# Expert work on pairs of chunks with 256-column operands, in a graph layer with a mixture of experts

## The chip, the cores and the metric

The kernel runs on one core of a Trainium2 chip. The core has a matrix engine (TensorE, in the profile PE for its matmuls and PEld for its weight loads), VectorE (DVE), ScalarE (ACT), GpSimd (POOL), a queue engine (SyncE, SP), a software-addressed on-chip memory (SBUF) and a small accumulator memory for matmul results (PSUM). The metric is the device time of one execution in microseconds (us). Smaller is better.

## The reference

The input is `x` of 6250 nodes by 256 features and 100,000 directed edges (`src`, `dst`), sorted by `dst`. Two layers are added to `x`, one after the other:

```python
# layer 1: graph neighbours
h       = layernorm(x)
msg_sum = segment_sum(h[src], dst, num_segments=n)
deg     = segment_sum(ones, dst, num_segments=n)
agg     = msg_sum / max(deg, 1)
x       = x + concat([h, agg]) @ W.T + b
# layer 2: mixture of 8 experts, each token goes to its best 2
xn      = layernorm(x) * gamma + beta
top     = top_k(xn @ Wr + br, 2);  w = softmax(top)
for e in range(8):
    hid = gelu(xn @ W1[e] + b1[e])        # 256 -> 512
    y  += (hid @ W2[e] + b2[e]) * w_full[..., e]   # 512 -> 256
x       = x + y
```

All is in float32.

## The kernel before

**Edges.** The kernel first computes `z = layernorm(x) @ W_agg` and a few more columns for all nodes and stores it to `z_d` in device memory. The edges come as 784 tiles of 128 edges. For each tile, POOL fetches the 128 rows of `z_d` that the sources name, with one indirect DMA (`gather`, L601), into one of a ring of `XG` = 28 buffers `xg`. VectorE makes a 0/1 matrix `hot` which says to which node of the window each edge goes (L612, seven tiles at once), and TensorE multiplies both into the accumulator `pS` (`add_edges`, L618). Fourteen tiles (`C`) make a window, and there are 56 windows (`W`). At a window's end ACT copies `pS` out (`keep_sums`, L640). The gather of tile t + `XG` is written straight after tile t's matmul, so the ring is filled as far ahead as it is long, and POOL waits when TensorE has not yet read the slot.

**Chunks.** Four windows (`CW`) form a chunk; there are 14 chunks, in batches of 8, 5 and 1 (`BATCHES`). After a chunk's last window a chain of steps, `window_done`, is spread over the next 56 tiles by due times (`Steps`, `LateSteps` for chunks 10 to 12, `LastSteps` for chunk 13): the second layer norm, the routing, counts and ranks, a sort by matmuls with 0/1 matrices (`sort_tokens`, L705, with the evictions L708), `copy_runs` (L859), and `find_rows` (from L805), which works out where each token's two results will be. `copy_runs` puts the sorted tokens into the chunk's slots in the buffer `xe`: 128 slots per expert, and what does not fit goes to overflow slots of the batch. There are two slot buffers of `HS` columns, for even and odd chunks, and the copies are 448 in all, four per expert and chunk. `xe` is `SC` = 5056 columns wide.

**Experts.** `start_experts` turns a chunk into tasks (`expert_stages`). Two experts share a task group: `hidden` (L884) does W1 times the slots, 2 x 8 matmuls of 128 columns, in two tasks, and the gelu (L889) on 128 columns each; `result` (L897) does hidden times W2, 2 x 4 matmuls of 256 columns, the bias add (L901) and the store to `y_d` (L903). After a batch's last chunk come the tasks of its overflow tiles (`more_stages`, L927, L936, L945). A chunk has 64 hidden and 32 result matmuls. A float32 matmul shows as two passes in the profile.

**Order.** The kernel's text decides the order on each engine. After each edge tile `after(t)` runs the steps that are due, adds a pace to an account (0.72 nominal us per tile; 0.6 in the last 56 tiles; 1.2 or 2.0 in the turns behind the last tile) and takes tasks from the list while the account is above zero; a hidden task counts 2.0 and a result task 1.75. `sum_rows` handles the output: for each of 49 node tiles a load of the layer-1 result (L973), two gathers from `y_d` on POOL (L976), two weighted adds on VectorE (L983) and a store (L985). It starts in the last `XG` tiles, in slots of the ring that are no longer needed, three per node tile, and only for a batch whose experts are all done; at most `XG // 3 - 1` adds are pending.

Of the kernel before, what the change touches and what calls it, by code (L numbers as in the profile page):

```python
# [8 lines left out]
F32 = mybir.dt.float32  # L9
I32 = mybir.dt.int32  # L10
AF = mybir.ActivationFunctionType
ALU = mybir.AluOpType
# [5 lines left out]
P = 128  # L18
EPS = 1e-5
C = 14  # L20
TB = 4
UB = 2
CW = 4
CAP = 64
BATCHES = (8, 8), (5, 5), (1, 2)
GB = 3
LATE = 40
XG = 28
RAW = 1
LATE_CHUNKS = 4  # L30

# [2 lines left out]
def gnn_ffn_kernel(ctx: ExitStack, tc: tile.TileContext, x, x_cols, src, dst, dst_next, gw, gw_t, gb, gb_cols, gamma, beta,  # L34
# [35 lines left out]
    nc = tc.nc  # L70
    N, D = x.shape
    NX, H = w1.shape[0], w1.shape[2]
    KD, KH = D // P, H // P
# [3 lines left out]
    W = src.shape[1]  # L77
# [4 lines left out]
    SH = P  # L82
    HS = NX * SH + CAP
    XS = P + CAP
    SC = 2 * HS + XS * sum(n for _, n in BATCHES)

    class Group:
        pass
# [2 lines left out]
    batches = []  # L91
    for n, tiles in BATCHES:
        B = Group()
        B.first, B.n, B.tiles = sum(b.n for b in batches), n, tiles
        B.at = HS + XS * sum(b.tiles for b in batches)
        B.row = batches[-1].end_row if batches else 0
        B.more_row = B.row + n * NX * SH
        B.end_row = B.more_row + XS * tiles
        B.left = n * NX * SH // (2 * P) + tiles
        batches.append(B)  # L100
# [3 lines left out]
    ps = ctx.enter_context(tc.tile_pool(name="ps", bufs=2, space=PSUM))  # L104
# [3 lines left out]
    y_d = dram.tile([batches[-1].end_row, D], F32, name="y_d")  # L108
# [734 lines left out]

    def copy_runs(K, e):
        if e == 0:
            assert K.index < 2 or Ks[K.index - 2].left == 0
        lowest = min(K.at, K.batch.at)
        _, v = nc.values_load_multi_w_load_instructions(
            K.runs[0:1, e].rearrange("o j t -> o (j t)"), engines=(ET.Activation,),
            min_val=0, max_val=SC, skip_runtime_bounds_check_because="clamped to it")  # L850
        for j in range(CW):
            to_at = nc.s_assert_within(v[2 * j], lowest, K.last,
                                       skip_runtime_bounds_check_because="behind the base, and clamped")
            src_at = nc.s_assert_within(v[2 * j + 1], 0, 2 * P,
                                        skip_runtime_bounds_check_because="a window has so many at most")
            whole = xs[:, j * KD * 2 * P:(j + 1) * KD * 2 * P + CAP]
            src = bass.AP(tensor=whole.tensor, offset=whole.offset,
                          ap=[whole.ap[0], [2 * P, KD], [1, 2 * P + CAP]])
            nc.scalar.activation(xe[:, :, bass.ds(to_at, CAP)], src[:, :, bass.ds(src_at, CAP)], AF.Copy)  # L859
# [5 lines left out]
    def in_turn(items, of):  # L865

        return [(us, f, of) for t in range(len(items) + 2) for d in range(3)
                if 0 <= t - d < len(items) and d < len(items[t - d]) for us, f in items[t - d][d]]

    def expert_stages(K):  # L870

        B = K.batch

        def hidden(U, h):

            if h == 0:
                U.hid = slots.tile([P, KH, 2 * P], F32, name="hid")
            ph = ps.tile([P, KH // 2, 2 * P], F32, name="ph")
            for i in range(KH // 2):
                c = h * KH // 2 + i  # L880
                for a in range(2):
                    at = K.at + (U.e + a) * SH
                    for k in range(KD):
                        nc.tensor.matmul(ph[:, i, a * SH:(a + 1) * SH], w1_sb[:, U.e + a, k, c * P:(c + 1) * P],  # L884
                                         xe[:, k, at:at + SH], start=(k == 0), stop=(k == KD - 1))
            for i in range(KH // 2):
                c = h * KH // 2 + i
                for a in range(2):
                    nc.scalar.activation(U.hid[:, c, a * SH:(a + 1) * SH], ph[:, i, a * SH:(a + 1) * SH],  # L889
                                         AF.Gelu, bias=b1_sb[:, U.e + a, c:c + 1])  # L890

        def result(U, h):

            if h == 0:
                U.py = ps.tile([P, 2, D], F32, name="py", bufs=1)
            for c in range(KH):
                nc.tensor.matmul(U.py[:, h, :], U.hid[:, c, h * P:(h + 1) * P], w2_sb[:, U.e + h, c, :],  # L897
                                 start=(c == 0), stop=(c == KH - 1))
            if h == 1:
                ys = slots.tile([P, 2, D], F32, name="rows", bufs=3)  # L900
                nc.vector.tensor_tensor(ys, U.py, b2_sb[:, U.e:U.e + 2, :], op=ALU.add)  # L901
                at = K.row + U.e * SH
                nc.sync.dma_start(y_d[at:at + 2 * P, :].rearrange("(t p) d -> p t d", p=P), ys)  # L903
                K.left -= 1
                B.left -= 1

        items = []
        for e in range(0, NX, 2):
            U = Group()
            U.e = e  # L910
            items.append([[(2.0, lambda U=U, h=h: hidden(U, h)) for h in range(2)],
                          [(1.75, lambda U=U, h=h: result(U, h)) for h in range(2)]])
        K.left = len(items)
        return in_turn(items, K)

    def more_stages(B):
# [70 lines left out]

    tasks, later, Ks, sums, adds = [], {}, [], [], []  # L990
    slots, w1_sb, w2_sb, xe = None, None, None, None
    now, spent, clock, due, added, spares = None, 0.0, 0.0, 0.0, 0.0, 0
    class Steps:
# [61 lines left out]

    def start_experts(K):
        B = K.batch
        tasks.extend(expert_stages(K))
        if K.index == B.first + B.n - 1:
            tasks.extend(more_stages(B))  # L1060
        Ks.append(K)
        sums.extend((K, n) for n in K.nodes)
# [22 lines left out]
    def after(t):  # L1085
        nonlocal now, spent, clock
        now = t
        while later.get(t):
            later[t].pop(0)()
        later.pop(t, None)  # L1090
        clock += 0.6 if t < W * C else 0.3 if tasks else 1.2

        pace = 0.6 if W * C - 56 <= t < W * C else 0.72 if t < W * C else 1.2 if len(Ks) < W // CW else 2.0
        spent = min(spent + pace, pace) if tasks else 0.0
        while tasks and spent > 0:
            us, f, _ = tasks.pop(0)
            spent -= us
            clock += us
            f()
        sum_rows()  # L1100
# [15 lines left out]
    for index in range(W // CW):  # L1116
        K = Group()
        K.index, K.first = index, index * CW
        K.batch = next(B for B in batches if index < B.first + B.n)
        K.row = K.batch.row + (index - K.batch.first) * NX * SH  # L1120
        K.at = 0 if index % 2 == 0 else SC - HS
        K.last = max(K.at + HS, K.batch.at + XS * K.batch.tiles) - CAP
        K.count = work.tile([1, 2, CW, NX], F32, name="count")
        G = K.group = Group()
        G.n, G.first, G.x1 = CW, K.first, []
        G.mv = small.tile([P, CW, 2], F32, name="mv4", bufs=2)
        for g in range(K.first, K.first + CW):
            if g > 0:
                V = V_next
            for c in range(C):  # L1130
                t = g * C + c
                add_edges(V, c)
                if c == 0:
                    hot_tiles(V, HC)
                if c == HC and g + 1 < W:
                    V_next = new_window(g + 1, V)
                if t + XG < len(edge_tiles):
                    gather(*edge_tiles[t + XG])
                for to, what in loads[:1]:
                    loads.pop(0)  # L1140
                    nc.sync.dma_start(to, what)
                if u_tasks and t % 2 == 0:
                    u_tasks.pop(0)()
                    if not u_tasks:
                        u_pools.close()
                        slots = fast_pools.enter_context(tc.tile_pool(name="slots", bufs=2))
                        at(t + 60, load_last)
                        xe = slots.tile([P, KD, SC], F32, name="xe", bufs=1)
                        for n in range(4):
                            at(t + 3 + 5 * n, clear_slots, n)  # L1150
                        w1_sb, w2_sb, parts = weights(slots)
                        for n, (to, what) in enumerate(parts):
                            at(t + 2 + 2 * n, nc.scalar.dma_start, to, what)
                if c == HC + 5:
                    load_u(V)
                if c == C - 1:
                    window_done(V, G, K, t)
                after(t)
    t = W * C
# [152 lines left out]
```

## Time and profile before

| what | value |
|---|---|
| time, median of 3 runs | 1426.46 us (1421.05 to 1427.55) |
| profiled execution, its own time | 1418.08 us |
| span of the profiled execution | 1416.3 us |
| mean granted TensorE clock | 0.892 |
| TensorE busy (matmuls) | 1123.6 us, 79% |
| TensorE busy (weight loads) | 903.0 us, 64% |
| VectorE busy | 690.8 us, 49% |
| ACT busy | 460.5 us, 33% |
| POOL busy | 843.9 us, 60% |
| 784 edge tiles end at about | 1256 us |

The span runs from the first to the last instruction; the time of the profiled execution is 1.8 us longer. A line of a group gives the line of code, engine and operation, what is written and read, how often, then busy time, mean duration of one in ns, and the engine's idle time before these instructions with what ended most of it. `issue` means that the engine waited for nothing that the profile shows. The starts of expert work are visible in the timeline; ACT's eviction at L640 marks the end of each window but the last. Busy time of TensorE is modelled for pipelined matmuls, so a busy TensorE is not one at its peak.

### The profile page before, as it was taken

How to read it: one execution, taken by the hardware profiler on the slowest of the kernel's cores; microseconds unless marked ns; L12 is line 12 of the kernel's file. 1: busy time of each engine (PE TensorE's matmuls, PEld its weight loads, DVE VectorE, ACT ScalarE, POOL GpSimd, SP SyncE). 2: the span in 40 equal slices, each digit the busy share in tenths (PEclk: the TensorE clock that was granted, in tenths of full speed). 3: DMA queues.
4: the chain of work that ended last, by engine and by line, in shares of the span. 5: the costliest groups of instructions: out<-in, count | busy, mean ns of one | idle time of the engine just before them, and what ended most of it. 6: DMA issues, size and time to landing. Idle time of an engine off the chain costs nothing. (4 is left out here: it accounts for less than half of the span.)

```text
span 1416.3 us, 18881 instructions
## 1 busy us (share of the span) xinstructions
PE 1123.6 (79%) x5352; PEld 903.0 (64%) x5352; DVE 690.8 (49%) x2433; ACT 460.5 (33%) x1281; POOL 843.9 (60%) x892
## 2 busy tenths in 40 slices
PE   7819957696987879698796969899889897986760
PEld 6718734575766758586675857567767786774650
DVE  6637776163444435354443534555462643656423
ACT  3310003333342333344243323433542343532310
POOL 0256666666666666666666666566656666564543
PEclk9859977898998989899897988999999998997876
DMA  9858895445454454544445454454545453564754
GB/s 331 285 181 269 270 324 157 104 123 122 114 128 113 114 120 117 123 122 120 118 115 112 123 119 115 118 124 115 120 111 133 116 134 103 115 197 139 197 148 126
DMA packets 143578, 210.08 MB, mean 148 GB/s; under 512 B 36652, under 2 KB 111128, under 8 KB 143340
## 3 DMA queue, kind: packets, MB, share of 16 engines
q0 software_dynamic: 42768, 118.91, 34.3%
q1 hardware_dynamic: 92364, 80.45, 18.0%
q10 hardware_dynamic: 8336, 9.45, 2.0%
q8 instruction: 45, 0.74, 0.2%
q14 instruction: 65, 0.53, 0.1%
HBM read 163.86 MB, written 44.86 MB: 147 GB/s over the span
## 5 line engine op out<-in xcount | busy, mean ns | idle before, releaser
L601 POOL DMA_INDIRECT xg<-z_d,src_i x770 | 732.5, 951 | 415.2 <-issue 175.7
L618 PE MATMUL pS<-xg,hot 128*128 128x265 f32 x1568 | 452.4, 418 | 68.8 <-DVE hot L612 33.4
L618 PEld LDWEIGHTS pS<-xg,hot 128*128 128x128 f32 x1568 | 304.8, 204 | 151.7 <-issue 97.5
L884 PE MATMUL ph<-xe,w_sb 128*128 128x128 f32 x1792 | 255.4, 293 | 75.5 <-issue 66.3
L884 PEld LDWEIGHTS ph<-xe,w_sb 128*128 128x128 f32 x1792 | 243.1, 207 | 94.8 <-issue 77.4
L612 DVE TENSOR_TENSOR hot<-cols,rel 128x896 f32<-128x896 f32 x112 | 121.9, 1089 | 275.5 <-PE pS L618 154.3
L897 PE MATMUL py<-w_sb,hid 128*128 128x256 f32 x896 | 223.2, 391 | 28.0 <-issue 16.8
L889 ACT ACTIVATE hid<-ph,b_sb 128x128 f32<-128x128 f32 x448 | 126.4, 374 | 270.4 <-remote 125.5
L897 PEld LDWEIGHTS py<-w_sb,hid 128*128 128x128 f32 x896 | 172.2, 195 | 64.5 <-issue 36.4
L859 ACT ACTIVATE xe<-xs x448 | 139.3, 311 | 86.3 <-issue 36.4
L976 POOL DMA_INDIRECT xg<-y_d,plans x98 | 95.7, 977 | 83.1 <-issue 21.4
L901 DVE TENSOR_TENSOR rows<-py,b_sb 128x512 f32<-128x512 f32 x56 | 38.5, 688 | 168.9 <-PE py L897 62.7
L708 ACT ACTIVATE xs<-pm,beta_sb,gamma_sb 128x256 f32<-128x256 f32 x112 | 57.2, 566 | 169.2 <-PE pm L705 73.7
L705 PE MATMUL pm<-to,xn 128*128 128x256 f32 x224 | 62.5, 403 | 24.6 <-DVE to L698 18.7
L640 ACT ACTIVATE sums<-pS 128x265 f32<-128x265 f32 x55 | 21.4, 389 | 172.1 <-PE pS L618 100.2
L705 PEld LDWEIGHTS pm<-to,xn 128*128 128x128 f32 x224 | 44.1, 201 | 35.6 <-issue 11.6
L271 PE MATMUL ph<-gc,x_t 128*128 128x264 f32 (+1 forms) x200 | 58.8, 420 | 8.2 <-ACT root L180 4.2
L889 ACT ACT_TABLE_LOAD x25 | 32.1, 1283 | 77.8 <-PE pS L618 43.5
L271 PE MATMUL pm<-gc,x_t 128*128 128x264 f32 (+1 forms) x192 | 54.9, 411 | 0.0
L271 PEld LDWEIGHTS ph<-gc,x_t 128*128 128x128 f32 x200 | 40.2, 205 | 18.6 <-ACT root L180 4.6
L983 DVE SCALAR_TENSOR_TENSOR xg<-xg,plans,xg 128x256 f32<-128x256 f32 (+1 forms) x98 | 45.4, 482 | 12.5 <-DMA xg<-y_d,plans 10.9
L660 DVE SCALAR_TENSOR_TENSOR x<-pS,rdeg,x 128x264 f32<-128x264 f32 x55 | 27.1, 493 | 48.1 <-DMA x<-u_d 35.4
(214 smaller groups left out, 873.4 us busy)
## 6 DMA issues: line engine op xcount, KB each, us to landing
y_d<-rows SPq DMA_DIRECT2D x56, 256.0 KB
xg<-z_d,src_i POOLq DMA_INDIRECT x770
w_sb<-w_dram ACTq DMA_DIRECT2D x16, 512.0 KB
x<-u_d SPq DMA_DIRECT2D x55, 132.0 KB
x_d<-x SPq DMA_DIRECT2D x55, 128.0 KB
u_d<-u_t SPq DMA_DIRECT2D x24, 264.0 KB
x_t<-x_cols_dram SPq DMA_DIRECT2D x12, 512.0 KB
xu<-x_dram SPq DMA_DIRECT2D x24, 256.0 KB
```

Of the source, the lines that this page charges most:

```text
L271: nc.tensor.matmul(pz, x_t[:, t, k, :], gc[:, h * KD + k, :n], start=(k == 0), stop=(k == KD - 1))
L601: nc.gpsimd.indirect_dma_start(out=xg[(g * C + c) % XG][:, :DZ], out_offset=None, in_=z_d[:, :], in_offset=bass.IndirectOffsetOnAxis(ap=sr ...
L612: nc.vector.tensor_tensor(hot, col[:, None, :].to_broadcast([P, HC, P]), V.rel[:, c:c + HC, None].to_broadcast([P, HC, P]), op=ALU.is_equal)
L618: nc.tensor.matmul(V.pS, V.hot[c // HC][:, c % HC, :], xg[(V.g * C + c) % XG], start=(c == 0), stop=(c == C - 1))
L705: nc.tensor.matmul(px[:, k, :], G.xn[i][:, k * P:(k + 1) * P], G.one_hot[i], start=True, stop=True)
L708: nc.scalar.activation(xs[:, at:at + 2 * P], px[:, k, :], AF.Identity, bias=beta_sb[:, k:k + 1], scale=gamma_sb[:, k:k + 1])
L859: nc.scalar.activation(xe[:, :, bass.ds(to_at, CAP)], src[:, :, bass.ds(src_at, CAP)], AF.Copy)
L884: nc.tensor.matmul(ph[:, i, a * SH:(a + 1) * SH], w1_sb[:, U.e + a, k, c * P:(c + 1) * P], xe[:, k, at:at + SH], start=(k == 0), stop=(k = ...
L889: nc.scalar.activation(U.hid[:, c, a * SH:(a + 1) * SH], ph[:, i, a * SH:(a + 1) * SH], AF.Gelu, bias=b1_sb[:, U.e + a, c:c + 1])
L897: nc.tensor.matmul(U.py[:, h, :], U.hid[:, c, h * P:(h + 1) * P], w2_sb[:, U.e + h, c, :], start=(c == 0), stop=(c == KH - 1))
L976: nc.gpsimd.indirect_dma_start(out=V.y2[r], out_offset=None, in_=y_d[:K.batch.end_row, :], in_offset=bass.IndirectOffsetOnAxis(ap=plans[:c ...
L983: nc.vector.scalar_tensor_tensor(V.o, V.y2[r], plans.bitcast(F32)[:count, n, 2 + r:3 + r], V.o, op0=ALU.mult, op1=ALU.add)
```

## The change

Chunks 0 to 11 are worked on in six pairs (`PAIRS`), by a new `pair_stages`; chunks 12 and 13 stay alone.

- A pair becomes tasks when its odd chunk's experts start. The even chunk's tasks wait until then, 56 tiles longer than before.
- `hidden` does one expert of both chunks: the 128 slots of the one and the 128 of the other are a single operand of 256 columns in two segments. Per expert that is 8 matmuls of 256 columns, in place of 16 of 128, and 4 gelus of 256 columns in place of 8 of 128. `result` keeps its count and size; its two halves are now the same expert of two chunks, so that the bias is one row for both, and the store is one DMA to two blocks of rows.
- `xe` holds three slot buffers: one for odd chunks, two which even chunks take in turn (chunks 12 and 13 go on in that turn). The overflow slots of the last batch share the place of the first's. `SC` becomes 5760. The ring `XG` goes from 28 to 24 buffers.
- A task counts 1.75, and the pace is 0.8 while more than 16 tasks are waiting, otherwise 0.72, in the tiles before the last 56.

```diff
--- before.py
+++ after.py
@@ -25,7 +25,8 @@
 BATCHES = (8, 8), (5, 5), (1, 2)
 GB = 3
 LATE = 40
-XG = 28
+XG = 24
+PAIRS = 6
 RAW = 1
 LATE_CHUNKS = 4
 
@@ -82,7 +83,10 @@
     SH = P
     HS = NX * SH + CAP
     XS = P + CAP
-    SC = 2 * HS + XS * sum(n for _, n in BATCHES)
+    OVER = 2 * HS
+    RIGHT = OVER + XS * (BATCHES[0][1] + BATCHES[1][1])
+    SC = RIGHT + HS
+    assert len(BATCHES) == 3 and BATCHES[2][1] <= BATCHES[0][1]
 
     class Group:
         pass
@@ -92,7 +96,7 @@
     for n, tiles in BATCHES:
         B = Group()
         B.first, B.n, B.tiles = sum(b.n for b in batches), n, tiles
-        B.at = HS + XS * sum(b.tiles for b in batches)
+        B.at = OVER if len(batches) == 1 else OVER + XS * BATCHES[1][1]
         B.row = batches[-1].end_row if batches else 0
         B.more_row = B.row + n * NX * SH
         B.end_row = B.more_row + XS * tiles
@@ -843,7 +847,8 @@
 
     def copy_runs(K, e):
         if e == 0:
-            assert K.index < 2 or Ks[K.index - 2].left == 0
+            assert K.at not in filled or filled[K.at].left == 0
+            filled[K.at] = K
         lowest = min(K.at, K.batch.at)
         _, v = nc.values_load_multi_w_load_instructions(
             K.runs[0:1, e].rearrange("o j t -> o (j t)"), engines=(ET.Activation,),
@@ -913,6 +918,58 @@
         K.left = len(items)
         return in_turn(items, K)
 
+    def pair_stages(K, L):
+
+        B = K.batch
+        assert L.batch is B and L.at < K.at
+
+        def slots_of_both(k, e):
+
+            own = xe[:, k, L.at + e * SH:L.at + (e + 1) * SH]
+            return bass.AP(tensor=own.tensor, offset=own.offset, ap=[own.ap[0], [K.at - L.at, 2], [1, SH]])
+
+        def hidden(U, h):
+
+            if h == 0:
+                U.hid = slots.tile([P, KH, 2 * P], F32, name="hid")
+            ph = ps.tile([P, KH // 2, 2 * P], F32, name="ph")
+            for i in range(KH // 2):
+                c = h * KH // 2 + i
+                for k in range(KD):
+                    nc.tensor.matmul(ph[:, i, :].rearrange("p (t s) -> p t s", t=2),
+                                     w1_sb[:, U.e, k, c * P:(c + 1) * P], slots_of_both(k, U.e),
+                                     start=(k == 0), stop=(k == KD - 1))
+            for i in range(KH // 2):
+                c = h * KH // 2 + i
+                nc.scalar.activation(U.hid[:, c, :], ph[:, i, :], AF.Gelu, bias=b1_sb[:, U.e, c:c + 1])
+
+        def result(U, h):
+
+            if h == 0:
+                U.py = ps.tile([P, 2, D], F32, name="py", bufs=1)
+            for c in range(KH):
+                nc.tensor.matmul(U.py[:, 1 - h, :], U.hid[:, c, h * P:(h + 1) * P], w2_sb[:, U.e, c, :],
+                                 start=(c == 0), stop=(c == KH - 1))
+            if h == 1:
+                ys = slots.tile([P, 2, D], F32, name="rows", bufs=3)
+                nc.vector.tensor_tensor(ys, U.py, b2_sb[:, U.e:U.e + 1, :].to_broadcast([P, 2, D]), op=ALU.add)
+                first = y_d[K.row + U.e * SH:K.row + (U.e + 1) * SH, :]
+                both = bass.AP(tensor=first.tensor, offset=first.offset,
+                               ap=[first.ap[0], [(L.row - K.row) * D, 2], first.ap[-1]])
+                nc.sync.dma_start(both, ys)
+                K.left -= 1
+                L.left -= 1
+                B.left -= 1
+
+        items = []
+        for e in range(NX):
+            U = Group()
+            U.e = e
+            items.append([[(1.75, lambda U=U, h=h: hidden(U, h)) for h in range(2)],
+                          [(1.75, lambda U=U, h=h: result(U, h)) for h in range(2)]])
+        K.left = L.left = len(items)
+        return in_turn(items, K)
+
     def more_stages(B):
 
         def one(T):
@@ -987,7 +1044,7 @@
 
 
 
-    tasks, later, Ks, sums, adds = [], {}, [], [], []
+    tasks, later, Ks, sums, adds, filled = [], {}, [], [], [], {}
     slots, w1_sb, w2_sb, xe = None, None, None, None
     now, spent, clock, due, added, spares = None, 0.0, 0.0, 0.0, 0.0, 0
     class Steps:
@@ -1055,7 +1112,10 @@
 
     def start_experts(K):
         B = K.batch
-        tasks.extend(expert_stages(K))
+        if K.index >= 2 * PAIRS:
+            tasks.extend(expert_stages(K))
+        elif K.index % 2:
+            tasks.extend(pair_stages(Ks[-1], K))
         if K.index == B.first + B.n - 1:
             tasks.extend(more_stages(B))
         Ks.append(K)
@@ -1090,7 +1150,7 @@
         later.pop(t, None)
         clock += 0.6 if t < W * C else 0.3 if tasks else 1.2
 
-        pace = 0.6 if W * C - 56 <= t < W * C else 0.72 if t < W * C else 1.2 if len(Ks) < W // CW else 2.0
+        pace = 0.6 if W * C - 56 <= t < W * C else (0.8 if len(tasks) > 16 else 0.72) if t < W * C else 1.2 if len(Ks) < W // CW else 2.0
         spent = min(spent + pace, pace) if tasks else 0.0
         while tasks and spent > 0:
             us, f, _ = tasks.pop(0)
@@ -1118,7 +1178,12 @@
         K.index, K.first = index, index * CW
         K.batch = next(B for B in batches if index < B.first + B.n)
         K.row = K.batch.row + (index - K.batch.first) * NX * SH
-        K.at = 0 if index % 2 == 0 else SC - HS
+        single = index - 2 * PAIRS
+        if single < 0 and index % 2:
+            K.at = 0
+        else:
+            K.at = (HS, RIGHT)[(index // 2 if single < 0 else PAIRS + single) % 2]
+        K.left = NX
         K.last = max(K.at + HS, K.batch.at + XS * K.batch.tiles) - CAP
         K.count = work.tile([1, 2, CW, NX], F32, name="count")
         G = K.group = Group()
```

## The prediction

> **What bounds the kernel now.** I read the groups of instructions first, then the evictions of the segment sums, which mark the end of each window, then the timeline of one chunk's start, then the stretches after the last edge tile. The costliest groups of the page (busy us, mean ns of one, then idle before them and its releasers):
>
> ```profile
> L601 POOL DMA_INDIRECT xg<-z_d,src_i x770 | 732.5, 951 | 415.2 <-issue 175.7
> L618 PE MATMUL pS<-xg,hot 128*128 128x265 f32 x1568 | 452.4, 418 | 68.8 <-DVE hot L612 33.4
> L884 PE MATMUL ph<-xe,w_sb 128*128 128x128 f32 x1792 | 255.4, 293 | 75.5 <-issue 66.3
> L897 PE MATMUL py<-w_sb,hid 128*128 128x256 f32 x896 | 223.2, 391 | 28.0 <-issue 16.8
> ```
>
> One matmul shows as two passes. A pass of the edges costs 452.4/1568 = 0.2885 us of TensorE, a hidden pass of 128 columns 255.4/1792 = 0.1425, a result pass of 256 columns 223.2/896 = 0.2491. POOL's gathers come at best 0.951 + 0.30 = 1.25 us apart, so a window of 14 tiles takes 17.5 us at least. The timeline of ACT has one eviction per window; here are the ends of windows 7 and 11, and of 23 to 27:
>
> ```profile
> 262.44 0.39 ACT L640 ACTIVATE sums<-pS 128x265 f32<-128x265 f32 x1 [9.06 <-remote]
> ...
> 345.10 0.39 ACT L640 ACTIVATE sums<-pS 128x265 f32<-128x265 f32 x1 [6.89 <-PE pS L618]
> ...
> 591.66 0.40 ACT L640 ACTIVATE sums<-pS 128x265 f32<-128x265 f32 x1 [5.06 <-issue]
> 616.10 0.37 ACT L640 ACTIVATE sums<-pS 128x265 f32<-128x265 f32 x1
> 636.36 0.39 ACT L640 ACTIVATE sums<-pS 128x265 f32<-128x265 f32 x1
> 657.54 0.39 ACT L640 ACTIVATE sums<-pS 128x265 f32<-128x265 f32 x1 [5.69 <-PE pS L618]
> 676.34 0.39 ACT L640 ACTIVATE sums<-pS 128x265 f32<-128x265 f32 x1 [7.85 <-remote]
> ```
>
> Windows 24 to 27 take 24.4, 20.3, 21.2 and 18.8 us. By the order of the instructions they hold 32 hidden matmuls; 16 hidden and 16 results; 16 and 12; 4 results. So the last is near POOL's 17.5, and the others are TensorE's: the second has 28 x 0.2885 + 32 x 0.1425 + 32 x 0.2491 = 20.6 us of passes. The first has only 8.1 + 64 x 0.1425 = 17.2 and takes 24.4. What it loses is in the timeline of TensorE (start, us, what, idle before):
>
> ```profile
> 667.22 3.90 PE L618 MATMUL pS<-xg,hot 128*128 128x265 f32 x8 [3.75 <-issue]
> 670.92 2.76 PE L884 MATMUL ph<-xe,w_sb 128*128 128x128 f32 x16
> ...
> 675.62 0.27 PE L884 MATMUL ph<-xe,w_sb 128*128 128x128 f32 x1 [0.83 <-issue]
> ...
> 679.12 0.27 PE L884 MATMUL ph<-xe,w_sb 128*128 128x128 f32 x1 [2.42 <-issue]
> ```
>
> A gap, then passes far apart with no wait that the profile shows. After the last edge tile (about 1256 us) comes a tail of 160 us; busy time of all engines by stretch, then of the hidden and of the result line alone:
>
> ```profile
> core 0: us, PE busy (x) PEld busy (x) DVE busy (x) ACT busy (x) POOL busy (x), PEclk, DMA share, GB/s
> 1256.00:1305.00 49.00, 34.24 (x159) 26.60 (x158) 34.00 (x115) 16.18 (x38) 25.79 (x27) 0.83 0.56 168
> 1305.00:1334.00 29.00, 24.67 (x132) 19.98 (x133) 17.08 (x55) 17.30 (x61) 13.78 (x15) 0.94 0.72 193
> 1334.00:1360.00 26.00, 11.69 (x49) 7.70 (x49) 3.33 (x7) 0.32 (x2) 16.87 (x18) 0.65 0.48 143
> ```
>
> ```profile
> 1256.00:1416.00 160.00, 24.50 (x190) 23.92 (x189) 0.78 0.55 161
> ```
>
> ```profile
> 1256.00:1416.00 160.00, 33.45 (x112) 23.48 (x112) 0.78 0.55 161
> ```
>
> The third stretch is slow as the chunk's start is:
>
> ```profile
> 1342.08 0.59 PE L897 MATMUL py<-w_sb,hid 128*128 128x256 f32 x1 [1.06 <-issue]
> 1344.17 0.58 PE L897 MATMUL py<-w_sb,hid 128*128 128x256 f32 x1 [1.50 <-issue]
> ```
>
> **The change, part by part.**
>
> *Wider hidden matmuls.* Two chunks have 256 hidden passes of 128 columns; a pair has 128 of 256. By the rows' means that is 36.5 against 31.9 us, 4.6 saved per pair, 27.6 for six. The trace has no such hidden pass, so it is bounded. Where passes stand tight (32 hidden in 3.73 us from 1322.27, 16 results in 3.62 us from 1331.03) it is 29.8 against 29.0: 5 us in all. With the idle time before them (0.1847 and 0.2804 a pass) it is 47.3 against 35.9: 68 in all. I take 27.6, since pair passes will lie among edges as results do.
>
> *Chunk 0 waits for chunk 1.* Windows 8 to 11 lose their expert work, 17.77 us of hidden and 15.30 of result passes in that stretch, 33.1 together. They take 345.10 - 262.44 = 82.7 us; without it POOL holds them at 4 x 17.5 = 70, or 72 by window 27's rate. I take 71: -11.7. The 33.1 us go to windows 12 to 55.
>
> *The end of the main loop.* Chunk 12 waits behind the pairs. Before, the tail has 190 hidden and 112 result passes, of which chunk 13 is 128 and 64; so 66 hidden and 16 result passes of chunk 12 run before it. In the changed order all of chunk 12 lies in the tail, and 12 result matmuls (24 passes) of the last pair: 66 x 0.1425 + 16 x 0.2491 + 24 x 0.2491 = 19.4 us leave the main loop.
>
> *Main loop, sum.* Windows 12 to 55: +33.1 - 27.6 - 19.4 = -13.9; with -11.7 that is -25.6. Twelve starts of a chunk's hidden work in a row become six, evenly mixed with results. A start costs some 5 us (24.4 against about 20 for windows with more work). But each chunk still has its row search (L805 and on) ahead of the next `hot` (L612), so the gap may stay: between 0 and -30, I take -5. Against that, where a pair's work is done after 128/24 = 5.3 windows, 2.7 of 8 run at POOL's rate instead of 2; their unused TensorE time is (17.5 - 9.1) x 2.7 = 22 against 2 x (17.5 - 10.1) = 15 per pair, at worst +30 over four pairs. I take 0, as TensorE can eat into the ring there. About -30; the ends are +27 (tight passes, all the waste) and -96.
>
> *Tail.* +19.4 of TensorE work. Node sums of batch 1 and their gathers on POOL (L976) can only start once chunk 12 is done, so POOL waits for it too. At the low end the 49.0 - 34.24 = 14.8 us idle in its first stretch cover it: +5. At the high end 16 result passes meet a stretch as from 1338.5 to 1361.2, 22.7 us in place of 3.6: +38. I take +16, since chunk 13's work queues directly behind.
>
> *Ring of 24, gelu, copies, stores.* Gathers for edges end four tiles later, 4 x 1.25 = 5 us, and one node tile less may be pending: 0 to +5, I take 0, since POOL is busy for 79 of the tail's 160 us. In the main loop the landing times in the trace lie over 20 us ahead of use, which covers four tiles fewer; without that cover each tile would add up to 1.25. ACT has per pair 64 gelus of 374 ns, then 32 wider ones, by the 256-column L708 row 566 ns: 23.9 against 18.1, hidden, as ACT is 33% busy. VectorE's bias add keeps its size, the store its bytes (256 KB), as one DMA per expert on SP. With the moved work go the four stores of chunk 0 and of chunk 12 and their 688 ns adds: chunk 12's pass onto SP's queue ahead of the tail's loads of x1 and onto VectorE ahead of the node sums, 4 x 0.7 = 2.8 us of VectorE, which is busy for 76 of the tail's 160 us and so has room; without it the tail grows by those 2.8. Copies into slots stay 448; the third buffer lets them run while a pair is worked on.
>
> *A rule against it.* In the stretch from 672 to 695 us, after the gap of 3.75 us, the granted clock is 0.76, and 1.00 from 695 to 716; the sum above lets it stay so. The Trainium skill ("TensorE: Matmul & The Clock Gate", the section on the HAM clock gate) states that the clock halves after about 3.4 us idle and needs about 3.4 us of work to return. By it the longer stretches without experts would each hold more such gaps, about 1.7 us of lost work apiece as an estimate from that page; with two more per pair, 20 us more, and the change would come out 6 us slower.
>
> *Sum.* -30 + 16 = -14. The profiled execution is 1418.08 us (span 1416.3), so 1404; the median, 1426.46, lies 8.4 above it, so 1412 on its footing.
>
> **Rivals.**
> 1. *The starts are the cost.* Hidden passes lose most by waiting for nothing shown (66.3 us of 75.5), and half the passes and half the starts go: -30 for starts in place of -5: 1387. Against it: result passes stall alike at 1342.
> 2. *The tail eats it (slower).* Chunk 12's work meets the slow stretch beside POOL's node gathers, as at 1342: +38 in place of +16, and 1434. It decides as soon as the tail grows by more than 30 + 7.
> 3. *POOL's floor eats it (slower).* The unused time at the floor is not regained: +30 in the main loop, which then gains nothing, and the tail's 16 stay: 1442. Against it: windows 10 and 11 take 17.0 and 18.1 in a row without the ring running dry.
> 4. *Nothing moves.* Saving and tail cancel: 1426.
>
> **How the numbers follow.** A measurement of this kernel tells about 0.5%, 7 us, from no change. Chances: forecast 0.42 (0.32 of it faster, 0.08 same, 0.02 slower); rival 1, 0.16, faster; rival 2, 0.18, and 3, 0.14, slower but for 0.02 and 0.02 that fall within 0.5%; rival 4, 0.10 (0.02 faster, 0.04 same, 0.04 slower). That is 0.50 faster, 0.16 same, 0.34 slower. The forecast's own range is 1390 to 1425. The whole range reaches past rival 1 to 1376, for passes dearer than their mean row, and past rival 3 to 1452.
>
> **What would show it.** Windows 8 to 11 should take about 71 us in all. The hidden group should have 768 pair passes at about 0.25 us each beside 256 of the old form. The last edge tile should end near 1226, and the tail take about 176. The forecast is wrong if the windows with pair work take over 22 us each, if the free ones stay above 18, if more than 20 us of `issue` idle stand before the result passes of the tail, or if `hot` becomes the wait at chunk ends.

## The result and the profile after

The changed kernel takes 1445.54 us (median of 4 runs, 1442.88 to 1449.5) beside 1427.01 us of the kernel before on the same chip: 1.0121 times as long, with a 95% interval of 1.0082 to 1.0159. The forecast was 1412 us. The profiled execution took 1442.88 us, its span 1441.1, 24.8 longer than before.

The costliest groups of the changed kernel's page answer to those shown of before:

```profile
L605 POOL DMA_INDIRECT xg<-z_d,src_i x770 | 733.0, 952 | 423.2 <-issue 167.8
L622 PE MATMUL pS<-xg,hot 128*128 128x265 f32 x1568 | 449.1, 417 | 113.4 <-issue 68.2
...
L939 PE MATMUL ph<-xe,w_sb 128*128 128x256 f32 x768 | 198.5, 404 | 35.1 <-ACT hid L944 14.8
...
L951 PE MATMUL py<-w_sb,hid 128*128 128x256 f32 x768 | 191.9, 391 | 19.1 <-issue 13.9
```

The hidden matmuls are as forecast: 768 passes of 198.5/768 = 0.258 us. But TensorE's idle time before the edge matmuls went from 68.8 to 113.4 us: the stalls moved to another line. ACT's evictions mark the window ends; here are those of windows 7 and 11 and of 23 to 27:

```profile
254.13 0.39 ACT L644 ACTIVATE sums<-pS 128x265 f32<-128x265 f32 x1 [4.29 <-issue]
...
340.18 0.39 ACT L644 ACTIVATE sums<-pS 128x265 f32<-128x265 f32 x1 [4.23 <-remote]
...
588.74 0.39 ACT L644 ACTIVATE sums<-pS 128x265 f32<-128x265 f32 x1 [2.05 <-PE pS L622]
608.65 0.38 ACT L644 ACTIVATE sums<-pS 128x265 f32<-128x265 f32 x1
630.49 0.39 ACT L644 ACTIVATE sums<-pS 128x265 f32<-128x265 f32 x1
645.91 0.39 ACT L644 ACTIVATE sums<-pS 128x265 f32<-128x265 f32 x1 [1.35 <-remote]
670.49 0.39 ACT L644 ACTIVATE sums<-pS 128x265 f32<-128x265 f32 x1 [10.02 <-PE pS L622]
```

Windows 8 to 11 have almost no expert work now (8 hidden passes, 2.7 us, at their very end), and take 340.18 - 254.13 = 86.1 us; with it they took 82.7. Windows 24 to 27 take 81.8, before 84.7. Over the stretch from window 8 to the last eviction, busy time of the engines before and after:

```profile
262.00:1242.00 980.00, 831.53 (x4115) 676.34 (x4116) 456.03 (x1619) 367.84 (x1023) 622.92 (x657) 0.92 0.48 118
```

```profile
254.00:1238.00 984.00, 803.59 (x3269) 626.94 (x3268) 453.60 (x1615) 332.34 (x817) 624.19 (x658) 0.91 0.46 117
```

The first number after the length is TensorE: 28 us less of work, in 4 us more. Behind the last eviction, the stretches of chunk 13's expert work (columns as in the prediction):

```profile
core 0: us, PE busy (x) PEld busy (x) DVE busy (x) ACT busy (x) POOL busy (x), PEclk, DMA share, GB/s
...
1341.00:1356.00 15.00, 14.25 (x108) 13.58 (x107) 4.92 (x11) 4.58 (x16) 7.58 (x8) 1.00 0.50 147
1356.00:1387.00 31.00, 7.07 (x15) 4.00 (x15) 4.38 (x10) 0.00 (x0) 21.26 (x23) 0.57 0.52 154
```

TensorE is full for 15 us, then does 15 passes in 31 us, while POOL gathers one row block after the other (22 start in that time, most of them 1.25 us apart). In TensorE's timeline:

```profile
1371.15 0.58 PE L902 MATMUL py<-w_sb,hid 128*128 128x256 f32 x1 [3.13 <-DVE xg L1040]
1373.98 0.59 PE L902 MATMUL py<-w_sb,hid 128*128 128x256 f32 x1 [2.25 <-issue]
1376.78 0.59 PE L902 MATMUL py<-w_sb,hid 128*128 128x256 f32 x1 [2.21 <-issue]
```

I call such stretches slow stretches: passes or other instructions far apart, put down to `issue`.

Where the 24.8 us of span come from follows from the evictions (us from the start of the span; "start" is up to eviction 7, "loop" from there to the last eviction at window 54, "tail" from there to the end):

| kernel and run | start | loop | tail | span |
|---|---|---|---|---|
| before, first profile | 262.4 | 979.9 | 174.0 | 1416.3 |
| before_same | 257.8 | 998.5 | 175.1 | 1431.4 |
| before_2 | 262.4 | 986.8 | 171.9 | 1421.0 |
| after, first profile | 254.1 | 984.4 | 202.6 | 1441.1 |
| after_same | 253.6 | 982.8 | 203.4 | 1439.7 |

By the means (before 260.8, 988.4, 173.7; after 253.9, 983.6, 203.0) the start gains 7, the loop gains 5, which is less than the before profiles differ among themselves, and the tail loses 29. That sums to 17, beside 18.5 between the medians.

### The profile page after: what moved, and what is told of

The parts are those of the page before. It is cut to its first block, busy times and chain, and to the rows that moved or that the text cites. A ratio compares the mean times of both kernels' runs of the same rounds, so it can differ in the third digit from the quotient of the medians.

```text
span 1441.1 us, 17238 instructions
## 1 busy us (share of the span) xinstructions
PE 1107.7 (77%) x4584; PEld 865.4 (60%) x4584; DVE 691.6 (48%) x2425; ACT 429.6 (30%) x1087; POOL 845.0 (59%) x892
## 4 chain that ended last, share of the span: by engine, by line
PE 52%; DVE 14%; issue 11%; another core or an unknown queue 9%; ACT 3%; DMA 2%; ACTq 1%; POOL 0%; DVEq 0%; SPq 0%; POOLq 0%
PE pS L622 17%; PE ph L939 12%; PE py L951 10%; PE pm L709 3%; PE py L902 2%; DVE hot L616 2%; PE py L1002 2%; PE ph L984 2%; PE pS L625 1%; ACT xe L864 1%; DMA xg<-y_d,plans 1%; DVE xg L1040 1%; DVE u_t L420 1%; DVE u_t L412 1%
## 5 line engine op out<-in xcount | busy, mean ns | idle before, releaser
L622 PE MATMUL pS<-xg,hot 128*128 128x265 f32 x1568 | 449.1, 417 | 113.4 <-issue 68.2
L622 PEld LDWEIGHTS pS<-xg,hot 128*128 128x128 f32 x1568 | 313.4, 205 | 202.8 <-issue 103.7
L939 PE MATMUL ph<-xe,w_sb 128*128 128x256 f32 x768 | 198.5, 404 | 35.1 <-ACT hid L944 14.8
L951 PE MATMUL py<-w_sb,hid 128*128 128x256 f32 x768 | 191.9, 391 | 19.1 <-issue 13.9
L939 PEld LDWEIGHTS ph<-xe,w_sb 128*128 128x128 f32 x768 | 153.1, 202 | 66.2 <-issue 27.2
L951 PEld LDWEIGHTS py<-w_sb,hid 128*128 128x128 f32 x768 | 149.3, 196 | 46.6 <-issue 23.9
L944 ACT ACTIVATE hid<-ph,b_sb 128x256 f32<-128x256 f32 x192 | 79.5, 472 | 249.2 <-PE pS L622 97.4
L709 PE MATMUL pm<-to,xn 128*128 128x256 f32 x224 | 69.0, 438 | 48.9 <-DVE to L701 24.0
L955 DVE TENSOR_TENSOR rows<-py,b_sb 128x512 f32<-128x512 f32 x48 | 33.1, 690 | 138.4 <-PE pS L622 59.3
L644 ACT ACTIVATE sums<-pS 128x265 f32<-128x265 f32 x55 | 21.5, 391 | 144.3 <-PE pS L622 99.9
L1040 DVE SCALAR_TENSOR_TENSOR xg<-xg,plans,xg 128x256 f32<-128x256 f32 (+1 forms) x98 | 45.9, 481 | 22.7 <-DMA xg<-y_d,plans 20.9
L902 PE MATMUL py<-w_sb,hid 128*128 128x256 f32 x128 | 38.0, 448 | 24.1 <-issue 12.1
L889 PE MATMUL ph<-xe,w_sb 128*128 128x128 f32 x256 | 35.1, 291 | 19.4 <-issue 11.2
```

The source lines that it names most:

```text
L622: nc.tensor.matmul(V.pS, V.hot[c // HC][:, c % HC, :], xg[(V.g * C + c) % XG], start=(c == 0), stop=(c == C - 1))
L709: nc.tensor.matmul(px[:, k, :], G.xn[i][:, k * P:(k + 1) * P], G.one_hot[i], start=True, stop=True)
L939: nc.tensor.matmul(ph[:, i, :].rearrange("p (t s) -> p t s", t=2), w1_sb[:, U.e, k, c * P:(c + 1) * P], slots_of_both(k, U.e), start=(k == ...
L944: nc.scalar.activation(U.hid[:, c, :], ph[:, i, :], AF.Gelu, bias=b1_sb[:, U.e, c:c + 1])
L951: nc.tensor.matmul(U.py[:, 1 - h, :], U.hid[:, c, h * P:(h + 1) * P], w2_sb[:, U.e, c, :], start=(c == 0), stop=(c == KH - 1))
L1040: nc.vector.scalar_tensor_tensor(V.o, V.y2[r], plans.bitcast(F32)[:count, n, 2 + r:3 + r], V.o, op0=ALU.mult, op1=ALU.add)
```

## The experiments

Two kinds of chip turned up. On four occasions (two of them on the same chip) the kernel before took 1415 to 1429 us; on two other chips, beside after_again and beside short3, 1194 and 1197 us. Times are compared with before on their own chip only, and I call the two kinds the slow and the fast chips. Noexp, noexp_same, nogather, spaced_2, pause7_2 and before_2 are single executions, and every run has one profile.

**The ring alone.**

```diff
-XG = 28
+XG = 24
```

> The kernel before with a ring of 24 gather buffers instead of 28, nothing else. Theory A (the ring is not what costs; the loss comes from chunk 12's work in the tail): within 0.5% of before, 1420 to 1434 us. Rival R (the shorter ring costs, since POOL can run less far ahead and one node tile less may be pending): 1438 us or more, which would be over half of the 18 us lost.

1414.65 beside 1415.49 us, 1.0012 (0.9977 to 1.0046). Its profile has start 250.5, loop 987.7, tail 177.5: the shorter ring starts the first window earlier, leaves the loop alone, and costs about 4 us in the tail. Rival R falls, and the 7 us that the changed kernel gains at the start fit the ring's.

**Five pairs instead of six.**

```diff
-PAIRS = 6
+PAIRS = 5
```

> The changed kernel with five pairs, so that chunks 10, 11 and 12 are worked on alone as before. Theory A (chunk 12 pushed behind the last edge tile by the last pair is what costs): the tail after the last window's eviction falls from 203 to 170 to 185 us, and the time to 1415 to 1430. Rival R (ring) and rival W (the wide matmuls or the pairs themselves are slow in the main loop): no gain of more than 7 us, 1438 or more.

1416.23 beside 1415.49 us, 1.0018 (0.9979 to 1.0056). The time is as theory A said, the tail is not: 187.5 us, above the 170 to 185. The loop is 974.1, shorter than any of before. Rivals R and W fall. On another slow chip, four runs side by side, the fourth of which is noexp_same below:

> The kernel before, profiled on the same chip as the next three. The two chips so far differ in the time of this one kernel (1415 and 1194 us). If this chip has no slow stretches: the loop runs at POOL's rate of 70 us per four windows from window 8 on, the last eviction comes before 1066 us (the changed kernel's there), and the tail is 140 to 155 us. If it has them: 81 to 85 us per four windows and a tail of 165 to 180.

1428.41 beside 1428.97 us, 1.0002 (0.9974 to 1.003): the kernel before against itself; four windows take 82 to 90 us, the tail 175.1.

> The changed kernel with five pairs, on the same chip as before_same. Theory A (the work of chunk 12 behind the last tile is the cost): within 1% of before on either kind of chip. Rival F (where POOL's rate binds the loop, the pairs themselves cost, since free and full stretches alternate): 1.5% or more slower than before on a chip without slow stretches.

1425.7 beside 1428.97 us, 0.9997 (0.9968 to 1.0026), with loop 975.7 and tail 192.6. Rival F was about chips without slow stretches and stays untried.

> The changed kernel on that same chip: 1.01 to 1.02 of before with slow stretches, 1.035 to 1.045 without.

1441.93 beside 1428.97 us, 1.0121 (1.0063 to 1.0178). So the sixth pair, and with it chunk 12 wholly behind the last tile, makes the loss: without it the loop gains some 13 us, the tail loses 16, and the time is that of before.

**No expert matmuls in the loop.** The matmuls and gelus of chunks 0 to 11 are left out; their stores write biases.

```diff
+            if K.index < 12:
+                return
             ph = ps.tile([P, KH // 2, 2 * P], F32, name="ph")
...
-            for c in range(KH):
+            for c in range(KH if K.index >= 12 else 0):
```

> The kernel before, without the matmuls and gelus of the experts for chunks 0 to 11 (their stores keep their places and hold biases). Theory B (the edge loop alone is not near POOL's floor: where POOL gathers back to back the other engines issue slowly and TensorE waits for hot, so taking expert work out of a window does not make it faster): windows 8 to 11 take over 78 us, and the last eviction comes at 1150 to 1230 us instead of 1242. Rival P (POOL's rate of 1.25 us a gather is the floor, as the prediction had it): windows 8 to 11 take 70 to 73 us, and the last eviction comes at 1080 to 1110.

1385.77 us, beside 1415.49. Windows 8 to 11 take 82.9 us, the loop 950.9; the last eviction comes at 1209.8. Theory B's numbers hold and rival P is far off. That the gathers are the reason, as B says, this run does not test.

> The kernel before without the experts' matmuls and gelus for chunks 0 to 11, on that same chip. Theory G (on a chip without slow stretches the gather rate alone bounds the loop): windows 8 to 51 take 70 to 73 us per four, as in the kernel before. If instead expert work bounds it there, they take 70 and the kernel before 75 or more. On a chip with slow stretches: 75 to 85 again.

On a slow chip, 1399.93 us beside 1428.97, the windows 68 to 85 us per four, the loop 965.2 against 998.5 of before_same. TensorE's busy time in this loop is 543 us instead of 847: some 300 us leave, and 33 us of time (noexp beside before_2, on one chip: 316 and 36). The granted clock in the loop fell as well, from 0.92 to 0.78, and the edge passes that stay take 416 us instead of 377; whether a full clock would have freed more time was not tried. What TensorE waits for now (engine, waited for, sum, times, longest):

```profile
PE pS L618 <- issue: 131.2, 23, 14.4
PE pS L618 <- DVE hot L612: 81.1, 15, 13.8
```

**What the others do in a slow stretch.** VectorE's timeline in the changed kernel, in a window without expert work, while POOL gathers from 269 to 293 us at 1.25 us each:

```profile
280.19 0.17 DVE L690 TENSOR_TENSOR q<-both,pm 128x32 f32<-128x32 f32 x1
281.66 0.19 DVE L691 TENSOR_TENSOR q<-q,place 128x32 f32<-128x32 f32 x1 [1.30 <-DVE q L690]
282.37 0.19 DVE L695 SCALAR_TENSOR_TENSOR mine<-rank,q 128x32 f32<-128x32 f32 x1 [0.52 <-DVE q L691]
284.48 0.19 DVE L696 TENSOR_REDUCE q<-mine 128x4 f32<-128x32 f32 x1 [1.92 <-issue]
```

Instructions of under 0.2 us start 1.47, 0.71 and 2.11 us apart. On a fast chip (after_again) the same four, while POOL gathers just as densely, start 0.20 to 0.23 us apart:

```profile
245.49 0.17 DVE L690 TENSOR_TENSOR q<-both,pm 128x32 f32<-128x32 f32 x1
245.69 0.19 DVE L691 TENSOR_TENSOR q<-q,place 128x32 f32<-128x32 f32 x1
245.92 0.19 DVE L695 SCALAR_TENSOR_TENSOR mine<-rank,q 128x32 f32<-128x32 f32 x1
246.14 0.18 DVE L696 TENSOR_REDUCE q<-mine 128x4 f32<-128x32 f32 x1
```

VectorE makes `hot` behind them, and in windows 8 to 11 TensorE waits 23.0 us for it:

```profile
PE pS L622 <- DVE hot L616: 23.0, 2, 12.2
PE pm L709 <- DVE to L701: 8.8, 1, 8.8
```

**Without the run of gathers beside chunk 13.** The adds of batch 1 take what lies in the buffers.

```diff
-        for r in range(2):
+        for r in range(2 if K.batch is not batches[1] else 0):
             nc.gpsimd.indirect_dma_start(
```

> The changed kernel without the node gathers of batch 1 (the adds take what lies in the buffers), so their long run beside chunk 13's matmuls is missing. Theory C (the slow passes of chunk 13, 31 us from 1356 to 1387, come from POOL gathering back to back): these passes run at their usual rate, without gaps for issue, and from chunk 13's first hidden matmul to its last result is under 30 us instead of 65. Rival D (TensorE is slow there for a reason of its own, clock or instruction supply): the gaps stay, and the stretch takes over 50 us.

1394.41 us, beside 1415.49 of before. Chunk 13's work, from its first hidden matmul, in TensorE's timeline:

```profile
1328.43 7.31 PE L889 MATMUL ph<-xe,w_sb 128*128 128x128 f32 x64
...
1339.03 3.73 PE L889 MATMUL ph<-xe,w_sb 128*128 128x128 f32 x32
1342.60 3.62 PE L902 MATMUL py<-w_sb,hid 128*128 128x256 f32 x16
...
1354.12 3.69 PE L902 MATMUL py<-w_sb,hid 128*128 128x256 f32 x16 [0.88 <-DVE rows L906]
```

It ends 29.4 us after it began, instead of 64.6 in the changed kernel (1341.56 to 1406.14), and no gap for `issue` is left. The gathers cause the slow stretch here; D falls. The time also lacks the gathers' own length at the end, so it is no price of the stretch.

**Is the spacing to blame, or the amount?** Twelve tiny clears on POOL after each node gather of batch 1:

```diff
+            if K.batch is batches[1]:
+                for _ in range(12):
+                    nc.gpsimd.memset(idle, 0.0)
```

> The changed kernel with twelve tiny clears on POOL after each node gather of batch 1, so that these gathers come about 2.5 us apart instead of 1.25. Theory C (back-to-back gathers make the other engines slow): chunk 13's matmuls run without gaps, 30 us instead of 64 from its first hidden matmul to its last result, though the gathers take twice as long. Rival D2 (the amount of gathered data, not its spacing): the gaps spread over the longer run of gathers and the stretch stays over 45 us.

This ran on a fast chip: 1317.93 beside 1194.39 us, 1.1036 (1.0999 to 1.1073). No slow stretch exists there with or without the spacing (in after_again's loop and tail no wait of TensorE for `issue` is as long as 0.5 us), so it tells nothing on C, but shows what lies next: TensorE waits up to 17.67 us for the bias adds (L907), which stand on VectorE's queue behind the node adds, which wait for the gathers.

> The changed kernel with twelve tiny clears after each node gather of batch 1. On a chip with slow stretches, theory C (close spacing of the gathers makes the other engines slow): while gathers run 2.5 us apart, no gaps of 0.7 to 2.2 us for issue stand between chunk 13's passes; what holds them is VectorE, whose bias adds queue behind node adds. Rival D2 (the gathers as such): the gaps for issue stay, over a longer time.

On a slow chip, 1502.1 beside 1427.76 us. In the timeline, with gathers 3.38 us apart:

```profile
1358.99 3.73 PE L890 MATMUL ph<-xe,w_sb 128*128 128x128 f32 x32
1373.87 5.40 PE L903 MATMUL py<-w_sb,hid 128*128 128x256 f32 x16 [11.14 <-DVE rows L907]
```

Sixteen or 32 passes in a row without a gap, and three waits of 11 to 18 us, all for VectorE's bias adds: with the same gathers, spaced, the slow stretch is gone. C holds, D2 falls, and the spacing itself costs far more than it frees: chunk 13's work takes 81.7 us.

**Breaking up the runs in the loop.** Ten clears after every seventh edge gather of the kernel before:

```diff
+        if (g * C + c) % 7 == 6:
+            for _ in range(10):
+                nc.gpsimd.memset(idle, 0.0)
```

> The kernel before with ten tiny clears on POOL after every seventh edge gather, about 1 us, so that no run of gathers is longer than seven; POOL's floor becomes about 1.4 us a gather, 78 us per four windows. Theory C in the main loop (long runs slow all engines down at each chunk's start): the gaps for issue ahead of the first window's hidden matmuls go and the last eviction comes earlier than 1242 by 10 us or more. Rival E (what starts the slow stretches is not the length of POOL's runs): the gaps stay, and the loop is as long or longer.

On a fast chip, 1393.0 beside 1194.39 us, 1.1665 (1.1628 to 1.1701); four windows take 83 to 88 us. By the profile ten clears take 1.53 us, so that seven gathers cost about 10.6 and four windows about 85: with POOL's floor lifted to there, the loop sits on it, and the gain expected where slow stretches occur could not show.

> The kernel before with about 1.5 us of tiny clears after every seventh edge gather. On a chip with slow stretches, theory C: the gaps for issue before hidden passes fall from 63 us to under 30, and the loop stays within 10 us of the kernel before or gets shorter. Rival E (the length of runs is not what starts them): the gaps stay at over 50 us. Without slow stretches: last eviction near 1231 us as before.

On a slow chip, 1443.76 beside 1427.76 us. The same four windows, 83 to 88 us. TensorE's waits in the loop:

```profile
PE pS L622 <- DMA xg<-z_d,src_i: 91.5, 88, 3.2
...
PE ph L888 <- issue: 3.7, 5, 1.2
```

and in the kernel before, as first profiled:

```profile
PE ph L884 <- issue: 63.3, 69, 2.5
```

The gaps for issue before hidden passes go (63.3 to 3.7 us), and gathered data is late in their place; those before edge passes stay (27.4 and 22.7). E falls for the hidden passes. The loop is 1005.3 us, 19 more than before_2's on the same chip, where I had said 10 at most. The fast chip's loop with these pauses was as long, 1005.0, as the raised floor would have it.

Two more things stand in this profile. Behind the last tile, where no pause was put, the gaps are there (pause7_2 from its last eviction on):

```profile
PE ph L888 <- issue: 32.0, 23, 3.1
```

And the start is 235.6 us, beside 262.4 of before_2, although POOL's floor is higher. In before_2, POOL gathers 17 times in a row up to 251.7 us, and VectorE stands still:

```profile
254.77 0.19 DVE L813 SCALAR_TENSOR_TENSOR q<-place,pm 128x32 f32<-128x32 f32 x1 [13.31 <-remote]
```

With the pauses the same instruction follows the one before it without a gap. So in the first eight windows breaking up the runs freed some 25 us, in one profile; the loop gave 19 back and the tail 29, counted against before_2.

> The kernel before, profiled beside the next three. With slow stretches (time near 1420): 81 to 85 us per four windows. Without (near 1195): about 70 us per four windows from window 8 on and the last eviction before 1066 us.

1422.8 us; four windows 82 to 89 us, tail 171.9. This too was a slow chip, the one of the three runs marked _2.

**Smaller pauses**, three clears or one, after every seventh edge gather and after every third node tile:

```diff
+        if c % 7 == 6:
+            pause()          # three clears, or one
```

> The kernel before with three tiny clears on POOL (about 0.46 us, with 0.3 more for the extra step) after every seventh edge gather and after every sixth node gather. POOL's floor is then (7 x 1.25 + 0.76) / 7 = 1.36 us a gather, 76 us per four windows. Theory C (long runs of gathers hold the loop): 77 to 80 us per four windows, hidden matmuls' gaps for issue under 30 us, and 1365 to 1400 us. Rival E (the loop is bound elsewhere, or so short a pause breaks nothing): 1415 or more. On a chip without slow stretches the floor alone decides: slower than before there.

> The same with one clear (0.15 us) in place of three: a floor of (7 x 1.25 + 0.45) / 7 = 1.31 us, 74 us per four windows. Theory C, if a pause of any length breaks a run: 75 to 79 us per four windows and 1345 to 1390 us, less than short3. If the pause must have a certain length: the gaps are back, and 1405 or more.

Both met a fast chip: short3 1282.09 beside 1196.71 us, 1.071 (1.0673 to 1.0747), at 74 to 79 us per four windows from window 12 on, as its floor says; short1 1193.97 us, 0.9971 (0.9951 to 0.9991). I had put short1's floor at 74 us, but its one clear fits between two gathers, which still start 1.25 us apart (407.53 and 408.78 us, the clear at 408.48): it is no pause at all. What they do to slow stretches was not seen, so whether a short pause makes the kernel faster on slow chips stays open. No run was clearly faster than both kernels.

**The width alone.** Order, buffers, pairs and gelus of the changed kernel, but the hidden matmuls at 128 columns:

```diff
-                    nc.tensor.matmul(ph[:, i, :].rearrange("p (t s) -> p t s", t=2),
-                                     w1_sb[:, U.e, k, c * P:(c + 1) * P], slots_of_both(k, U.e),
+                        nc.tensor.matmul(ph[:, i, a * SH:(a + 1) * SH], w1_sb[:, U.e, k, c * P:(c + 1) * P],
+                                         xe[:, k, own:own + SH], start=(k == 0), stop=(k == KD - 1))
```

> The changed kernel in its order of work, buffers and pairs, but each hidden matmul of 256 columns is two of 128, as before; the gelus stay at 256 columns. Theory B (TensorE's expert work is not what the main loop waits for): within 8 us of the changed kernel. The prediction's price (4.6 us per pair, 27.6 in all): 20 us or more slower than the changed kernel.

> The changed kernel itself, so that the run beside it has its own reference on the same chip: 1.008 to 1.016 of before.

These two ran on a fast chip: after_again 1242.46 beside 1194.39 us, 1.0395 (1.0362 to 1.0428), far above what I expected for it; narrow 1247.95 us, 1.0458 (1.043 to 1.0486). The width is worth 5.5 us there, within the 8 of theory B.

> The changed kernel with its hidden matmuls in two of 128 columns. Theory B (where slow stretches occur, TensorE's expert work is not what the loop waits for): 1.008 to 1.020 of before, like the changed kernel's 1.012. The prediction's price (27.6 us): 1.027 or more.

On a slow chip, 1456.43 beside 1427.76 us, 1.0217 (1.0131 to 1.0302), against 1.0121 of the changed kernel. That is some 14 us with an interval of about as much either way: neither nothing nor the 27.6 is excluded, and 1.0217 lies between the two ranges expected.

**Where the fast chip loses.** The profile of after_again has start 224.4, loop 842.2, tail 175.9; that of short1, 0.3% off the kernel before, 225.1, 822.7 and 146.8. So the tail costs 29 us there too, and the loop 20. In POOL's timeline of after_again gathers follow each other without end:

```profile
640.17 0.95 POOL L605 DMA_INDIRECT xg<-z_d,src_i  x1 [0.30 <-PE ph L939]
641.43 0.95 POOL L605 DMA_INDIRECT xg<-z_d,src_i  x1 [0.30 <-PE pS L622]
642.68 0.94 POOL L605 DMA_INDIRECT xg<-z_d,src_i  x1 [0.30 <-DMA xg<-z_d,src_i]
```

Here POOL's floor of 70 us per four windows is real. In short1 windows 12 to 35 take 66 to 71 us per four. In after_again they alternate, 74.2, 65.6, 74.8, 65.6 and so on, and each pair of fours sums to 140 to 141. Windows 8 to 11 take 61.5 (62.8 in short1, with expert work), less than the floor; POOL's lead in the ring would explain that. The loop's loss is at the end: windows 40 to 51 take 76.0, 75.4 and 82.1, beside 71.5, 70.6 and 72.4.

## Why the prediction was wrong, point by point

- **Windows 8 to 11, -11.7 us.** This step failed first. "Without it POOL holds them at 4 x 17.5 = 70, or 72" took POOL's best rate as what binds a stretch without experts. After the change they took 86.1 and 81.6 us in two profiles, and 82.9 and 84.0 in the runs without expert matmuls: nothing in place of -11.7. TensorE's work was not what held the loop there. On a slow chip VectorE and TensorE start late while gathers are dense, VectorE is late with `hot`, and TensorE waits for it. That the gathers cause this was shown behind the loop (nogather, spaced_2), for hidden passes in the loop and for the first eight windows (pause7_2); no run took them out of windows 8 to 11. On the fast chips the step was worth 1 us (61.5 beside 62.8).
- **TensorE passes as time, -13.9 us in windows 12 to 55.** The same failure. 28 us of TensorE's busy time left the loop and the idle time before edge matmuls took its place; the loop moved by 5 us instead of 30, within its spread. The runs without expert matmuls show how little such a step can bring: 300 us less of busy time were worth 33 us, at a lower clock.
- **The width, 27.6 us.** The passes came out as priced (0.258 against 0.249 us), but the width alone was worth 5.5 us on a fast chip, and on a slow one an amount that the interval hardly bounds. The change's other rows are as said: ACT 429.6 us busy instead of 460.5, VectorE as before.
- **Starts, -5 us.** The wait for `issue` before hidden passes did fall, from 63.3 to 11.0 us in the loop. Other waits of TensorE in the loop rose: for `hot` to 32.7 us from nothing (12.9 in after_same), for `to` to 21.5 from 9.0, for `issue` before result passes to 13.9 from 2.5. Rival 1, which priced these gaps as a gain, erred as the forecast did. The timeline lines from 667.22 us on, shown for the first of windows 24 to 27, belong to the next chunk's start; window 24's own gaps, from 593 to 605 us, are of the same kind and sum to 7.6 us.
- **The tail, +16 us.** Mechanism right, size short: +29. Counted from the last eviction, chunk 13's first hidden matmul came 23.1 us later (79.9 to 103.0 us), beside 19.4 of moved work. Chunk 13's work then took 64.6 us instead of 52.8 (1322.27 to 1375.04), in a longer slow stretch: batch 1's node gathers, released later, run beside it 30 in a row, before 22. What follows it is 6.3 us shorter. So the idle time that was to cover a part of the moved work seems to have covered none. Rival 2 named this place and this price, up to 38; but its -30 for the loop was missing too, so it gave 1434.
- **Rival 3**, POOL's floor eating the gain, gave 1442 us, close to the measured time, by luck: its reason holds only on the fast chips. There the alternating fours show it; on the slow ones eight windows take 162 to 168 us, and the floor of 140 is not reached.
- **The ring, 0.** Right for the sum only: +4 in the tail and 7 to 10 us less at the start, which I had not foreseen.
- **The clock rule.** The Trainium skill ("TensorE: Matmul & The Clock Gate", the HAM clock gate) holds that long idle gaps halve the clock. In windows 8 to 11 the granted clock did fall, to 0.76, 0.67, 0.89 and 0.70, from 0.93 before. It does not account for the time: TensorE was busy for 46.7 of these 86 us. Over the loop the clock was 0.91 beside 0.92, and over the whole run 0.89 as before, so the 20 us that the prediction set against itself by this rule are not seen.

What stays open: why dense gathers make other engines start instructions late on some chips and not on others, how short a pause breaks this, whether pauses can make the whole kernel faster on slow chips, and whether chunk 12 can be paired without going behind the last tile.

## What to carry to other kernels

Take an engine's work out of the loop entirely, in a throwaway kernel, before pricing a change that shortens it: here 300 us of busy time were worth 33. Idle time put down to `issue` on several engines at once points to a common cause, and work that leaves can then be replaced by waiting. And ask of anything deferred in a pipelined loop which of it now lies behind the last iteration, where nothing covers it.

## What the runs showed of the hardware

On the slow chips, while POOL issues indirect gathers 1.25 us apart, passes on TensorE and small instructions on VectorE start 0.7, 1.4 or 2.1 us apart. In the three tails looked at (before, after, pause7_2) TensorE's gaps begin 9.0 to 9.5 us, seven or eight gathers, into such a run. Leaving the gathers out, or spacing them 3.4 us, removes it in the tail, and a pause of 1.5 us after every seventh cuts the gaps before hidden passes in the loop from 63.3 to 3.7 us. On two other chips runs of gathers as dense, and longer, did nothing of the kind, and the same kernel took 1194 instead of 1427 us. One clear of 128 x 1 elements on POOL takes 0.10 us and, in a row, 0.15.
